# A cross-attention kernel whose engine calls are reissued in the order of a table, with 205 transfers on the other of two queues

## The chip, the cores and the metric

The kernel runs on one core of a Trainium2 chip. A core has a matrix engine (TensorE; PE in the profile, with PEld for its weight loads), a vector engine (VectorE, DVE), an activation engine (ScalarE, ACT), a general engine (GpSimd, POOL) and a synchronising engine (SyncE, SP) that here only issues transfers. Each takes its own instructions in order, and semaphores hold an instruction until what it needs is there. The metric is the device time of one execution in microseconds; smaller is better.

## The reference

A layer norm, a query projection, attention of 32 heads of width 32 over a context that serves as keys and as values, an output projection and a residual. Eight batches of 256 rows, model width 1024, all in float32:

```python
x = (hidden_states - mu) * jax.lax.rsqrt(var + LN_EPS) * ln_gamma + ln_beta
Q = _split_heads(x @ Wq.T)
scores = jnp.einsum('bhsd,bhtd->bhst', Q, K) * scale
scores = jnp.where(mask, scores, -jnp.inf)
probs = jax.nn.softmax(scores, axis=-1)
attn = jnp.einsum('bhst,bhtd->bhsd', probs, V)
out = attn @ Wout.T
return residual + out
```

## The kernel before

**Steps.** The loop (from L1204) has 64 steps `n`: eight batches by eight groups of four heads. Step `n` issues `scores(n + 1)` (L646), 8 matmuls of 32 rows of the array each, into the four tiles of the pool `ps_s`. `values` and `values_pair` (L823, L830) multiply the softmax of an earlier step with the values, 32 or 64 matmuls of 64 rows and 32 columns, into `ps_v`. Between them stand pieces of full-array work: query projections `pq` (`make_q` L504 with 256 columns; for batches 3 and up `query_product` L605, 16 matmuls of 128 columns for each of seven products, a Strassen-like scheme) and output projections `po` (`product_steps` L912, 512 columns). `pq` tiles live in `ps_q`, and `po` tiles mostly in `ps_o`; each of these pools has one buffer, so the next tile waits until ACT or DVE has copied the last one out. A table `PLAN` at the head of the file says at which step each load, sum and projection piece is issued.

**Softmax of a step** (`softmax_parts`, L670). For each head `j` and half `s` of the rows: DVE adds the mask and takes the minimum (L694), ACT takes the exponential and its sum (L698), DVE the reciprocal `rden` (L708). POOL multiplies (L714), or ACT for 52 of the 256 heads (L712). DVE transposes 32x32 blocks into `pT` (L720), ACT copies a part of them aside into `pc` (L726). Four transfers inside the chip then swap parts of `pT` (L800): two `pT<-pT`, and two `pT<-pc` that go back and wait for the first two. `values` reads the result.

**Head.** Thirty-two transposes of an identity (`busy`, L246) run while the first data arrive. The four quarters of `x` for batch 0 are the first loads on SP (`load_x`, L271), then `wq` block by block (`load_wq`, L333). DVE takes statistics of the quarters (L399), POOL raises to the power -1/2 (L407), DVE normalises (L425), PE transposes (L439), ACT and DVE copy (L448, L450), and `first_q` (L452, matmuls at L458) starts the projections.

**Tail.** After the loop the products of the last batch are added up (`end_steps`, matmuls at L997; `end_add`, L1003) and stored by `end_store` (L1353, issued at L1354), the last piece as 128 rows of 128 columns.

**Order and queues.** The whole body runs in a manual schedule (L241): every engine receives its instructions in the order in which Python makes the calls, and semaphores are derived from the same order. The identity and two small constants are written by POOL ahead of that line. `issue` (L254) puts a transfer on SP, or by `PLAN['qp']` on POOL at once or at the end of the step (L1337):

```python
        if mode == 0 or not in_loop:
            nc.sync.dma_start(to, of)
        elif mode == 1:
            nc.gpsimd.dma_start(to, of)
        else:
            at_end.append(partial(nc.gpsimd.dma_start, to, of))
```

Numbered in this order, the calls from L246 on are 6932: 3613 on PE, 1189 on DVE, 1016 on ACT, 636 on POOL (75 of them transfers) and 478 on SP (all transfers). On PE, a float32 matmul call becomes two weight loads and two matmuls.

Of the kernel before, what the change touches and what calls it, by code (L numbers as in the profile page):

```python
# [159 lines left out]
 'head': 1,  # L160
 'tail63': 1}

# [2 lines left out]

# [14 lines left out]
LN_EPS = 1e-5  # L180
MASKED = 3.0e38
NO_SCORE = 1.0e38


@with_exitstack
def xattn_kernel(
# [11 lines left out]
    nc = tc.nc  # L198
# [471 lines left out]
    def softmax_parts(n, copies=(), ahead=(), between=(), hooks={}, fill=()):  # L670
# [16 lines left out]
        def exps(j, part=range(NS)):  # L687
# [5 lines left out]
            for s in part:  # L693
                nc.vector.tensor_tensor_reduce(  # L694
                    out=e[:, s, :], in0=pss[j][:, s, :], in1=mbs[n // NQ], scale=1.0,
                    scalar=NO_SCORE, op0=ALU.add, op1=ALU.min, accum_out=mn[:, s : s + 1],
                )
# [312 lines left out]
    for n in range(N):  # L1010
        k = 0 if n == NQ + 1 else min(1, NQ * SPLIT - made)
# [14 lines left out]
    for b in range(1, B):  # L1026
        first = NQ * (b - 1) + 2
# [156 lines left out]
    for b in range(B - 1):  # L1184
        done, ends = 0, b == B - 2
# [19 lines left out]
    for n in range(N):  # L1205
        b, i = divmod(n - NQ, NQ)
# [194 lines left out]
    for cols in (first_cols, last_cols):  # L1401
# [2 lines left out]
        end_add(r01[:, cols], po)  # L1404
        end_store(0, 1, cols)


# [38 lines left out]
```

## Time and profile before

| | |
|---|---|
| median of 3 runs | 573.66 us (573.0 to 575.04) |
| span of the profiled execution | 572.0 us |
| instructions | 20001 |
| DMA engines | 116.93 MB, mean 204 GB/s |
| transfers issued by SP, packets' share of 16 engines | 55.2% |
| transfers issued by POOL, packets' share of 16 engines | 15.1% |

The span runs from the first to the last instruction of the profiled execution; no other time of that execution is given, and the lowest of the three runs lies 1.0 us above it. Rows of the profile read: line, engine, operation, what it writes `<-` what it reads, shapes and count, then busy time and mean duration in nanoseconds, then the idle time just ahead of these instructions with what ended most of it. A timeline row begins with its start and its length in us. A row of waits reads "who waited <- for whom: us in total, times, longest". A row of transfers ends with the size of one and the median time from issue to landing in us. "issue" is time in which an engine waited for nothing that the profile shows. Ends of matmuls are modelled; their starts are recorded.

### The profile page before, as it was taken

The page shows a single profiled execution, that of the slowest core. Times are in us where ns is not written, and L with a number is a line of the kernel's source. Part 1 is how long each engine was busy: PE and PEld are TensorE (multiplying, and loading weights), DVE is VectorE, ACT ScalarE, POOL GpSimd, SP SyncE. Part 2 cuts the span into 40 slices and gives each one's busy share as a digit, 9 for nine tenths or more (in the row PEclk, how much of TensorE's full clock was granted, in tenths as well). Part 3 has the DMA queues.
Part 4 walks back from the last instruction along what each step waited for, and adds up shares of the span by engine and source line. Part 5 has one row for each costly group of instructions (what it writes and reads, how often), then busy time and mean ns, then how long its engine had stood idle before and what let it go on. Part 6 is the DMA issues. An engine that isn't in the chain of part 4 may idle for free.

```text
span 572.0 us, 20001 instructions
## 1 busy us (share of the span) xinstructions
PE 562.9 (98%) x7162; PEld 394.6 (69%) x7162; DVE 466.2 (81%) x1701; ACT 450.5 (79%) x1527; POOL 399.1 (70%) x643
## 2 busy tenths in 40 slices
PE   8999999999999999999999999999999999999998
PEld 7788775767667677667675777667766777755454
DVE  5988899988878888988788987898877878688833
ACT  3699978888779877888768988789868888879920
POOL 1478978887678895787667774686955875267690
PEclk9999999999999999999999999999999999999999
DMA  8768778576777677877888677767866765547551
GB/s 298 278 174 252 203 206 230 133 205 189 203 235 203 205 207 220 257 210 205 214 249 234 206 201 221 229 200 209 233 189 193 226 182 175 145 136 228 153 167 74
DMA packets 45891, 116.93 MB, mean 204 GB/s; under 512 B 9136, under 2 KB 9904, under 8 KB 45792
## 3 DMA queue, kind: packets, MB, share of 16 engines
q1 hardware_dynamic: 38080, 90.14, 55.2%
q0 software_dynamic: 7424, 25.50, 15.1%
q8 instruction: 57, 0.93, 0.7%
q14 instruction: 42, 0.34, 0.2%
q10 hardware_dynamic: 288, 0.01, 0.0%
HBM read 64.23 MB, written 11.53 MB: 132 GB/s over the span
## 4 chain that ended last, share of the span: by engine, by line
PE 69%; DVE 9%; POOL 8%; ACT 6%; issue 4%; DMA 3%; SPq 0%; DVEq 0%; ACTq 0%; POOLq 0%
PE po_S L930 17%; PE pq_A L615 16%; PE sc L654 8%; PE pv L840 8%; PE po_A L930 8%; PE pq_S L615 6%; POOL e L714 5%; ACT e L698 3%; DVE e L694 3%; PE po_end L997 3%; DVE pT L720 3%; DMA pT<-pT 2%; ACT e L712 1%; PE pq L513 1%; DMA wq<-in_wq_dram 1%
## 5 line engine op out<-in xcount | busy, mean ns | idle before, releaser
L698 ACT ACTIVATE e<-e,mn 128x256 f32<-128x256 f32 x512 | 253.7, 502 | 32.8 <-DVE mn L694 30.2
L714 POOL TENSOR_SCALAR e<-e,rden 128x256 f32<-128x256 f32 x408 | 188.5, 476 | 125.0 <-DVE rden L708 116.8
L720 DVE STREAM_TRANSPOSE pT<-e 128x512 f32<-128x512 f32 x256 | 180.4, 707 | 54.6 <-POOL e L714 23.5
L694 DVE CUSTOM_DVE_ANT_0 e<-sc,mb 128x256 f32<-128x256 f32 x512 | 185.1, 415 | 13.0 <-PE sc L654 12.0
L726 ACT COPY pc<-pT 128x512 f32<-128x512 f32 x128 | 78.8, 617 | 43.7 <-DVE pT L720 28.5
L698 ACT ACTIVATION_READ_ACCUMULATOR e<-e,mn 128x1 f32 x512 | 98.9, 193 | 0.0
L513 PE MATMUL pq<-xnT,wq 128*128 128x256 f32 (+1 forms) x368 | 84.5, 383 | 0.0
L513 PEld LDWEIGHTS pq<-xnT,wq 128*128 128x128 f32 x368 | 68.6, 190 | 14.6 <-issue 3.4
L930 PE MATMUL po_S<-wo,at 128*128 128x512 f32 x152 | 73.5, 606 | 1.0 <-DVE r L972 0.7
L654 PE MATMUL sc<-k,qa 32*128 32x256 f32 x1024 | 73.8, 401 | 0.1
L654 PEld LDWEIGHTS sc<-k,qa 32*128 32x128 f32 x1024 | 45.9, 184 | 39.0 <-issue 17.8
L840 PE MATMUL pv<-pT,v_all 64*32 64x128 f32 x3584 | 61.0, 273 | 1.0 <-ACT e L712 0.6
L840 PEld LDWEIGHTS pv<-pT,v_all 64*32 64x32 f32 x3584 | 51.9, 105 | 12.8 <-issue 7.7
L930 PE MATMUL po_A<-wo,at 128*128 128x512 f32 x128 | 59.3, 604 | 0.1
L930 PE MATMUL po_S<-wo,s 128*128 128x512 f32 x104 | 49.9, 607 | 0.3 <-DVE rden L708 0.3
L708 DVE RECIPROCAL rden<-den 128x2 f32<-128x2 f32 x256 | 37.9, 148 | 13.1 <-ACT e L698 12.1
L712 ACT ACTIVATE e<-e,rden 128x256 f32<-128x256 f32 x104 | 46.8, 500 | 1.0 <-DVE rden L708 1.0
L615 PEld LDWEIGHTS pq_A<-xnT,wq 128*128 128x128 f32 x352 | 41.1, 192 | 5.6 <-issue 4.7
L930 PEld LDWEIGHTS po_S<-wo,at 128*128 128x128 f32 x152 | 26.0, 190 | 25.7 <-issue 23.9
L694 DVE DVE_READ_ACCUMULATOR2_ANT mn<- 128x1 f32 x512 | 42.3, 83 | 0.0
L615 PE MATMUL pq_A<-xnT,wq 128*128 128x128 f32 x352 | 41.2, 275 | 0.3 <-issue 0.3
L930 PEld LDWEIGHTS po_A<-wo,at 128*128 128x128 f32 x128 | 23.0, 189 | 26.5 <-issue 24.4
(116 smaller groups left out, 687.6 us busy)
## 6 DMA issues: line engine op xcount, KB each, us to landing
pT<-pT SPq DMA_DIRECT2D x128, 128.0 KB, 3.4
pT<-pc SPq DMA_DIRECT2D x128, 128.0 KB, 4.0
v_all<-in_kv_dram POOLq DMA_DIRECT2D x17, 512.0 KB, 4.8
k<-in_kv_dram SPq DMA_DIRECT2D x30, 256.0 KB, 4.2
r<-in_x_dram SPq DMA_DIRECT2D x26, 256.0 KB, 4.0
ring<-kept_T SPq DMA_DIRECT2D x11, 512.0 KB, 5.8
xnT<-xe SPq DMA_DIRECT2D x79, 64.0 KB, 3.9
out_dram<-r POOLq DMA_DIRECT2D x18, 256.0 KB, 3.7
```

What stands on the lines that cost most here:

```text
L513: nc.tensor.matmul(pqs[n], wq[:, o, c, :], xnTs[b](c), start=(c == 0), stop=(c == NC - 1),)
L615: nc.tensor.matmul(pqs[b][:, o, :], w[:, c], x_[:, c], start=begins and o + c == 0, stop=c == NK - 1, skip_group_check=True,)
L654: nc.tensor.matmul(scs[n][j][:, s, :], qa[r, n % NQ, ts(s, P)], ks[n - n % 2][r, n % 2, :], start=True, stop=True,)
L694: nc.vector.tensor_tensor_reduce(out=e[:, s, :], in0=pss[j][:, s, :], in1=mbs[n // NQ], scale=1.0, scalar=NO_SCORE, op0=ALU.add, op1=ALU.m ...
L698: nc.scalar.activation(e[:, s, :], e[:, s, :], AF.Exp, bias=mn[:, s : s + 1], scale=-1.0, accum_out=den[:, s : s + 1],)
L708: nc.vector.reciprocal(rden, dens[j])
L712: engine.activation(es[j][:, s, :], es[j][:, s, :], AF.Copy, scale=rden[:, s : s + 1])
L714: engine.tensor_scalar(es[j][:, s, :], es[j][:, s, :], rden[:, s : s + 1], 1.0, ALU.mult, ALU.mult,)
L720: nc.vector.transpose(pT[:, :, :, j, :, :].rearrange("p a i s k -> p (a i) s k"), es[j].rearrange("p s (b t) -> p b s t", t=K),)
L726: nc.scalar.copy(pc[:, :, ts(j, 2)], pT[:, 1, :, ts(j, 2)])
L840: nc.tensor.matmul(pvs[n][r][j * HD : (j + 1) * HD], vs[n - n % 2][ts(r, 2 * K), n % 2, i, ts(j, HD)], pT[ts(r, 2 * K), :, i, j, :, :], st ...
L930: nc.tensor.matmul(po, operand(b, name)[:, c], wo[:, which, c], start=begins and c == 0, stop=c == NK - 1, skip_group_check=not begins,)
```

## The change

Ahead of the kernel stand a table `ORDER`, a permutation of the numbers 0 to 6931 (runs written as `first-last`), and a dictionary `OTHER` of 205 call numbers with the engine that issues them instead. `Recorded` takes the place of `nc` right behind the manual schedule, keeps each call (engine, name, arguments) and issues none. After the last line of the body `issue` walks the table and makes the calls. The tiles are allocated in the same order as before, since Python runs the body as before. No call is added, left out or given other arguments.

By the table, against the old order of the same engine's calls, 1608 of 3613 calls on PE stand in another place, 950 of 1189 on DVE, 836 of 1016 on ACT, 443 on POOL and 260 on SP (of those that stay on their engine). A call on PE moves by at most 80 places.

Of the 205 transfers, 164 go from SP to POOL and 41 from POOL to SP:

| transfer | SP to POOL | POOL to SP |
|---|---|---|
| swaps `pT<-pT`, of 128 | 40 | 0 |
| swaps back `pT<-pc`, of 128 | 45 | 0 |
| blocks of x, `xnT<-xe` | 25 | 13 |
| keys `k`, values `v_all` and the last values in `wq` | 21 | 9 |
| residual rows `r` | 12 | 0 |
| `ring`, and `ring` kept in memory | 8 | 5 |
| weights `wq`, `wo` | 5 | 1 |
| rows `x`, mask | 3 | 2 |
| results `out` | 5 | 11 |

Among them are call 34, the first quarter of `x` for batch 0, and call 6931, the last store, both from SP to POOL.

```diff
+ORDER = """
+32-38 40 42 39 49 41 43-45 53-57 0-29 58-65 51 47 69-70 66-68 71-77 30-31 79-81 78 83-110 112 111 113 116-117
...
+6859 6904-6907 6898 6903 6913-6916 6806 6908-6911 6804 6917-6923 6902 6912 6924-6931
+"""
+OTHER = {
+    34: 'gpsimd', 46: 'gpsimd', 47: 'gpsimd', 48: 'gpsimd', 50: 'gpsimd', 51: 'gpsimd', 53: 'gpsimd',
...
+    6544: 'gpsimd', 6722: 'gpsimd', 6919: 'gpsimd', 6931: 'gpsimd',
+}
...
+class Recorder:
+    def __init__(self, engine, calls):
+        self.engine, self.calls = engine, calls
+
+    def __getattr__(self, name):
+        return lambda *a, **k: self.calls.append((self.engine, name, a, k))
+
+
+class Recorded:
+
+
+    def __init__(self, nc):
+        self.nc, self.calls = nc, []
+        for engine in ("tensor", "vector", "scalar", "gpsimd", "sync"):
+            setattr(self, engine, Recorder(engine, self.calls))
+
+    def __getattr__(self, name):
+        return getattr(self.nc, name)
+
+    def issue(self, order, other):
+
+        done = set()
+        for run in order.split():
+            first, *last = map(int, run.split("-"))
+            for i in range(first, (last[0] if last else first) + 1):
+                engine, name, a, k = self.calls[i]
+                getattr(getattr(self.nc, other.get(i, engine)), name)(*a, **k)
+                done.add(i)
+        assert len(done) == len(self.calls)
...
     ctx.enter_context(tc.manual_schedule())
+    nc = Recorded(nc)
...
+    nc.issue(ORDER, OTHER)
```

More of the change, by code (lines that the diff above doesn't have):

```diff
@@ new lines @@
+499 512 511 518 513-514 521 515 519 523-524 492 516-517 528 487 531-532 471-476 537-544 533 477-478 509 522
+591-592 525-527 529-530 536 535 593 598 390-391 485-486 488 490 545-576 534 577-579 581-582 580 583-588 597
+491 609 605-606 589-590 614 616 607-608 611 603-604 594 601-602 610 520 613 617 615 619-621 612 618 622 633
+596 595 600 599 637-680 717 624-626 623 627-631 697-698 632 689 685 687 696 699 686 690-693 688 709-710 704
+700 706 702 708 701 707 705 703 722 711-712 714 718-721 735-736 681-684 713 737 739 635 634 716 715 723 725
@@ new lines @@
+727 726 744-783 738 784 788-789 785-787 790-795 798 728 796 800 804 729 808-809 797 799 724 807 810 801 820
+817 811-813 815-816 845 839 842 695 848-850 945 732 802 949 636 694 740 818-819 741 829 822-823 814 825-826
+821 828 827 833 830-832 846-847 805 835 837 851-895 898-899 836 896-897 824 834 952-955 958 1034 909 838
+911-912 900-901 910 907 917-919 903 915-916 913-914 920-921 925 927-928 922-923 908 924 926 929-932 934-937
+956-957 959-966 1012 939 1016 1010 1039 1029 1217 841 803 904 1147 951 806 731 288 902 905 933 938 967-1009
@@ new lines @@
+5281 5330 5321-5322 5320 5318 5337-5339 5331 5336 5333 5332 5346 5342-5344 5355 5279 5334-5335 5340 5345
+5347-5348 5356-5432 5282 5141 5435 5454 5443-5444 5436-5438 5445 5447 5449-5451 5446 5452 5442 5453 5440 5448
+5456-5457 5441 5439 5341 5455 5459 5462 5472 5283 5484-5492 5434 5479 5460-5461 5483 5433 5458 5493-5509
+5511-5512 5463-5466 5468-5470 5482 5515-5516 5467 5471 5473-5474 5476 5286 5513-5514 5517 5519-5520 5518
+5526-5527 5523-5525 5530 5521-5522 5531 5528-5529 5535 5540 5534 5555-5556 5510 5546 5545 5547 5557 6455 5142
```

175 lines of the change are left out of this document (added).

## The prediction

> **What bounds the kernel now.** I read the cores' spans first, then busy times and the stretches of the span, then the matmul engine's waits, and only then the other engines and queues.
>
> ```profile
> core 0: 572.0 us, clock 1.000
> PE 562.9 (98%) x7162; PEld 394.6 (69%) x7162; DVE 466.2 (81%) x1701; ACT 450.5 (79%) x1527; POOL 399.1 (70%) x643
> ```
> ```profile
> 0.00:9.24 9.24, 6.66 (x40) 6.21 (x41) 4.49 (x10) 2.72 (x5) 1.47 (x9) 1.00 0.74 233
> 9.24:569.00 559.76, 556.00 (x7122) 388.36 (x7122) 461.39 (x1691) 447.75 (x1523) 397.67 (x635) 1.00 0.72 205
> 569.00:572.10 3.10, 0.19 (x2) 0.00 (x0) 0.29 (x1) 0.00 (x0) 0.00 (x0) 0.95 0.24 85
> ```
>
> The three stretches are the head (warm-up and first rows of x), the stream of matmuls, and the last store; the columns are length, busy PE, PEld, DVE, ACT, POOL, then clock, DMA share and GB/s. In the stream PE stands idle for 559.76 - 556.00 = 3.76 us, at full clock. The new table keeps every call, so it can take out idle time of PE, and move head and tail. It can't take out matmuls.
>
> ```profile
> 143.67 1.02 PE L930 MATMUL po_S<-wo,s 128*128 128x512 f32 x2
> 144.53 3.62 PE L513 MATMUL pq<-xnT,wq 128*128 128x256 f32 x16
> 148.81 1.13 PE L930 MATMUL po_S<-wo,at 128*128 128x512 f32 x2 [0.67 <-DVE r L972]
> ```
> ```profile
> 148.81 0.30 PEld L930 LDWEIGHTS po_S<-wo,at 128*128 128x128 f32 x2 [1.07 <-DVE r L972]
> PEld pq L513 <- issue: 3.4, 15, 0.3
> ```
>
> Here is one true stall (evacuation of `po_S` by DVE is late). PE shows 0.67 us. The weight loads, which otherwise pause 3.4 / 15 = 0.23 us in this group, pause 1.07, so the stall is about 0.84: the previous matmul's drawn end covers 0.17 of it. With the same cover of 0.17 on some 16 stalls in the stream, the 3.76 us become 3.76 + 16 x 0.17 = 6.5 us. Sixteen is a guess: the list of PE's waits names ten causes, two of them in the head. So the stall budget is 3.8 to 6.5 us; I take 6.5 as its whole size. The Trainium skill (Perfetto Trace Analysis, Tensor Engine Instruction) says that a matmul's end is estimated, not observed; the two rows at 148.81 agree. By drawn ends alone the budget would be 3.76 us.
>
> ```profile
> PE pq_A L615 <- issue: 1.3, 2, 1.0
> PE po_S L930 <- DVE r L972: 0.7, 1, 0.7
> PE pv L840 <- ACT e L712: 0.6, 1, 0.6
> ```
>
> Of it, 1.3 us (two pauses in `pq_A`) waits for nothing that the profile shows, and no order of ours addresses that. The addressable rest is at most 6.5 - 1.3 = 5.2 us, 0.9% of the span.
>
> **The change part by part.** I numbered the kernel's 6932 calls in the order it makes them, which is what the table's numbers mean, and counted. PE time between two calls is the sum, along an order, of each call's start-to-start time in the trace.
>
> *Order on PE.* 3613 calls, 1608 of them in another place. The 8 `scores` calls of a step and the 32 or 64 of `values` stay together; projection matmuls (`pq`, `po`) are cut into smaller pieces and spread. Stretches of small-tile work, each left and entered again, go from 69 to 71.
>
> ```profile
> 300.59 5.42 PE L930 MATMUL po_A<-wo,at 128*128 128x512 f32 x12
> 305.94 1.15 PE L654 MATMUL sc<-k,qa 32*128 32x256 f32 x16
> 307.02 1.98 PE L930 MATMUL po_A<-wo,at 128*128 128x512 f32 x4
> 308.84 3.40 PE L615 MATMUL pq_S<-sx,ring 128*128 128x128 f32 x29
> ```
>
> Each of these calls is two instructions. Six calls between two small-tile stretches take 305.94 - 300.59 = 5.35, two take 308.84 - 307.02 = 1.82 with one such border only. Four calls and a border are 3.53; at 0.86 a call (143.67 to 144.53 above) a border costs about 0.1, a stretch 0.2: two more cost 0.4 us. Cutting `pq` and `po` finer among each other costs nothing by these rows.
>
> What the cuts do is move waits. From the last `scores` matmul of a step to the first `values` matmul that needs its softmax, the PE time in between grows by over 0.5 us in 36 of 64 steps and shrinks by over 0.5 in 12 (at most 2.8). The one-buffer pool `ps_q` goes the other way: PE time between the last matmul into one tile and the first into the next was under 2 us once in 40, and is now in 11 (1.2 to 2.0). In that gap ACT must copy the tile out.
>
> ```profile
> L625 ACT ACTIVATE qa<-pq_S,qa 128x128 f32<-128x128 f32 x40 | 11.3, 366 | 0.4 <-PE pq_S L615 0.2
> L522 ACT ACTIVATE qa<-pq,qa 128x256 f32<-128x256 f32 x8 | 3.4, 462 | 0.0
> L698 ACT ACTIVATE e<-e,mn 128x256 f32<-128x256 f32 x512 | 253.7, 502 | 32.8 <-DVE mn L694 30.2
> ```
>
> A copy is 0.46 us, or 4 x 0.366 = 1.5 us for the four of a product, behind perhaps one exp of 0.5 us: it fits in 1.8 us where ACT comes to it at once, and is 0.2 us over where an exp and a product's four copies stand in line. Eleven such places cost 0 to 2.2 us; I take 1. Of the 5.2 us addressable I let the new distances remove 4.5, since they mostly lengthen. The stall term is -4.5 + 1 = -3.5 us; its ends are -5.2 (all addressable stalls gone) and +2.2 (none gone, all eleven late).
>
> *Order on DVE, ACT, POOL, SP.* 950, 836, 443 and 260 calls change place. Nothing is added; DVE at 81% and ACT at 79% hide behind PE as long as the distances above hold. I price it inside the stall term.
>
> *Transfers.* 164 go from SP to POOL, 41 back: 123 more on POOL, among them 85 of the 256 swaps of `pT` (L800).
>
> ```profile
> L261 POOL DMA_DIRECT2D v_all<-in_kv_dram x18 | 10.8, 600 | 0.0
> L1337 POOL DMA_DIRECT2D out_dram<-r x18 | 10.6, 586 | 0.3 <-issue 0.2
> L714 POOL TENSOR_SCALAR e<-e,rden 128x256 f32<-128x256 f32 x408 | 188.5, 476 | 125.0 <-DVE rden L708 116.8
> DVE pT L720 <- POOL e L714: 23.5, 67, 2.6
> ```
>
> 123 x 0.59 = 72.6 us more on POOL, 399.1 + 72.6 = 471.7 us (82%). It is hidden by POOL's 173 us of idle time, of which 116.8 wait for DVE's `rden`. If that cover is gone, the normalised `e` is late next, then DVE's transposes, the swaps and `values`.
>
> Two moved transfers have no cover. *Head:* the first quarter of x (call 34) goes from SP to POOL.
>
> ```profile
> 0.73 1.81 SPq L259 DMA_DIRECT2D x<-in_x_dram  x4
> 1.02 0.28 POOL masks.py:199 TENSOR_SCALAR_AFFINE_SELECT ring<-ring 128x128 f32<-128x128 f32 x1
> 3.58 1.47 DVE L399 BATCH_NORM_STATS2 st<-x 128x6 f32<-128x512 f32 x2 [3.58 <-DMA x<-in_x_dram]
> 9.24 0.57 PE L458 MATMUL pq<-xnT,wq 128*128 128x128 f32 x3 [1.04 <-DMA wq<-in_wq_dram]
> ```
> ```profile
> v_all<-in_kv_dram SPq DMA_DIRECT2D x7, 512.0 KB, 4.9
> v_all<-in_kv_dram POOLq DMA_DIRECT2D x17, 512.0 KB, 4.8
> r<-in_x_dram SPq DMA_DIRECT2D x26, 256.0 KB, 4.0
> r<-in_x_dram POOLq DMA_DIRECT2D x2, 256.0 KB, 6.5
> xnT<-xe SPq DMA_DIRECT2D x79, 64.0 KB, 3.9
> xnT<-xe POOLq DMA_DIRECT2D x17, 64.0 KB, 4.7
> out_dram<-x_again SPq DMA_DIRECT2D x1, 64.0 KB, 1.6
> ```
>
> DVE takes that quarter first in both orders. SP issued it at 0.73 and DVE began at 3.58. POOL is free at 1.30, 0.57 later, and from issue to landing a POOL transfer takes 0.8 us more (4.7 against 3.9), with ends -0.1 (4.8 against 4.9) and +2.5 (6.5 against 4.0). So DVE starts 1.4 us later (0.5 to 3.1). About 0.3 us of that is slack, because the first projection waited for `wq` too. After 9.24 PE has no idle time to absorb it: +1.1 us, ends +0.2 and +2.8. The Trainium skill (DMA: Bandwidth & Descriptors, Specifications) gives about 1 us to the first byte on GpSimd's path and 0.6 on SP's; the pair 4.7 and 3.9 agrees in sign. By an estimate from that page the head would cost 0.57 + 0.4 - 0.3 = 0.7 us. *Tail:* the last store (call 6931, 64 KB, 1.6 us on SP) is issued by POOL: by the same pairs +0.8 us, ends -0.1 and +2.5.
>
> *Sum* against the profiled execution: 572.0 - 3.5 (stalls) + 0.4 (stretches) + 1.1 (head) + 0.8 (tail) = 570.8 us. The median of the runs shown, 573.66, lies 1.7 above that span, so I forecast 570.8 + 1.7 = **572.5 us**. This case, stalls mostly gone and about half of that given back at both ends, spans 571.0 to 574.5.
>
> **The rivals.** *The table pays in full:* the 5.2 us go, head and tail hide (by the `v_all` pair, POOL is no slower). For it: 36 longer distances. Against: POOL is free 0.57 us late whatever the queue does. 573.66 - 5.2 + 0.4 = 568.9.
>
> *Stalls move, none goes:* each wait removed comes back in `ps_q`, stall term 0. For it: 11 gaps under 2 us with ACT 79% busy; against: ACT is reordered too. 573.66 + 2.3 = 576.0.
>
> *POOL becomes the bound (the slower side).* Place: a `pT` swap on POOL that stands ahead of `e` and waits.
>
> ```profile
> SPq L800 <- DMA pT<-pT: 103.8, 66, 5.3
> SPq L800 <- ACT pc L726: 55.5, 22, 4.2
> SPq L800 <- ACT e L698: 50.2, 25, 8.5
> SPq L800 <- ACT at L853: 34.6, 10, 7.4
> ```
>
> SP waits 244.1 us over 256 swaps, 0.95 each. If POOL waits as long for its 85, that is 81 us: 471.7 + 81 = 552.5. Head and tail, where POOL has nothing to do, are 10.9 us (9.24 - 1.47 and 3.10). It decides once POOL's remaining waits for `rden`, 116.8 us now, stay above 572.0 - 552.5 - 10.9 = 8.6 us. If a sixth stays (19.5), the span is 552.5 + 10.9 + 19.5 = 582.9, with the 1.7 around it 584.6. For it: behind 17 of the 45 returning swaps on POOL the table puts under 3 us of POOL work between the two swaps of a step, less than a landing. Against: 28 have more, and the longer PE distances allow it.
>
> *The order does not arrive:* if the instruction order of the program were remade behind the table, 573.7. Against: the kernel builds in a manual schedule, and today's trace follows its calls one by one.
>
> **How the numbers follow.** Forecast 0.38, full gain 0.17, stalls move 0.22, POOL bound 0.20, no effect 0.03. A measurement of this kernel tells about 0.3% (1.7 us) from no change: faster is below 571.9, slower above 575.4. Faster: 0.17 of the full gain and 0.17 of the forecast's lower part; same: 0.20 of the forecast, 0.03 of moved stalls, 0.03 of no effect; slower: 0.01, 0.19 and 0.20. So 0.34, 0.26, 0.40. The range 568.3 to 582.0 leaves out the upper part of the POOL case and the least of the full gain, under 0.2 together.
>
> **What would show it.** Stall term: PE idle in the long stretch near 1.5 to 2.5 us instead of 3.76, with `ps_q` copies named where it remains. Head: DVE's first statistics near 5.0 instead of 3.58, the first projection near 10.3 instead of 9.24. Tail: last matmul to end of span about 0.8 us longer. POOL busy near 472 us, PE still at full clock. I am wrong if PE idles more than 6 us in the stream, if waits for POOL's `e` grow well over 23.5 us on DVE, or if the first statistics start as early as now.

## The result, and the profile after

The changed kernel takes 592.38 us (median of 4 runs, 590.88 to 594.14), the kernel before 573.33 in the runs beside it: a ratio of 1.0318, with a 95% interval of 1.0273 to 1.0364. It is slower by about 19 us. Here and below, medians and ratios leave out executions that took over 1.5% more than the fastest of the same kernel: one of start_back (594.02 us) and one each of queues_only and both_back (about 1988 us, over twice the others, which nothing here explains). The profiled execution spans 591.2 us where the one of before spans 572.0.

First the spans and the busy time of the engines, from the view of cores and the page:

```profile
core 0: 591.2 us, clock 0.994
PE 573.6 (97%) x7162; PEld 401.6 (68%) x7162; DVE 460.1 (78%) x1701; ACT 452.5 (77%) x1527; POOL 464.8 (79%) x766
```

POOL has its 123 transfers more (x766 for x643) and 65.7 us more work. No engine but PE is near the span. Now the same three stretches as before the change, cut at the first projection and behind the last addition (columns: length, busy PE, PEld, DVE, ACT, POOL, clock, DMA share, GB/s):

```profile
0.00:11.55 11.55, 7.61 (x40) 7.13 (x40) 3.87 (x9) 1.79 (x3) 2.71 (x10) 1.00 0.76 268
11.55:588.00 576.45, 566.00 (x7122) 394.47 (x7122) 456.24 (x1693) 450.66 (x1525) 461.57 (x755) 0.99 0.69 197
588.00:591.30 3.30, 0.00 (x0) 0.00 (x0) 0.00 (x0) 0.00 (x0) 0.54 (x1) 1.00 0.21 76
```

The head is 11.55 - 9.24 = 2.3 us longer, the stream 576.45 - 559.76 = 16.7. In the stream PE is idle for 576.45 - 566.00 = 10.45 us (3.76 before), and "busy" for 10 us more on the same 7122 matmuls. A part of that is matmuls at half clock, in two windows of 3.4 us that the kernel before doesn't have:

```profile
96.97:100.38 3.41, 3.41 (x64) 2.27 (x65) 2.18 (x12) 2.46 (x8) 1.95 (x4) 0.51 0.56 129
455.40:458.80 3.40, 3.40 (x9) 1.24 (x5) 2.03 (x7) 3.17 (x13) 2.50 (x6) 0.50 0.64 212
```

They account for up to half of their 6.8 us, 3.4. The rest is drawn ends that cover stalls. So I also measured stalls by starts: for each run of like matmuls, the time from its start to the next run's start, less what undisturbed runs of that kind take in the trace of before (0.858 us a `po` call, 0.432 and 0.223 a `pq` call of 256 and 128 columns, 1.08 the scores of a step, 1.09 the values of one). Behind the first 16 us these excesses sum to 6.6 us before and 21.6 after: 15.0 us of new stalls, half clock included, in some two dozen places.

The waits that the prediction named, and the ones that grew most (engine and line, what it waited for, us in total, times, longest):

```profile
POOL e L410 <- DVE rden L410: 50.1, 61, 6.9
DVE rden L410 <- ACT e L410: 47.6, 78, 2.2
DVE pT L410 <- POOL e L410: 31.8, 54, 2.4
POOL pT L410 <- DMA pT<-pT: 15.5, 8, 5.7
```
```profile
DVE rden L708 <- ACT e L698: 12.1, 21, 1.0
```

The last row is of before. All calls now have one line, L410, because the helper issues them. DVE waits four times as long for ACT's exponentials, and POOL, which waited 116.8 us for `rden`, now waits 50.1 for it and is held by swaps instead.

How a stall comes about is best seen at two places. The first, from the timelines of SP and of PE:

```profile
85.23 0.58 SPq L410 DMA_DIRECT2D wo<-in_woT_dram  x1
85.91 0.58 SPq L410 DMA_DIRECT2D pT<-pT  x1
89.96 0.51 SPq L410 DMA_DIRECT2D pT<-pc  x1
90.56 0.53 SPq L410 DMA_DIRECT2D v_all<-in_kv_dram  x1
91.19 0.38 SPq L410 DMA_DIRECT2D k<-in_kv_dram  x1
91.62 0.51 SPq L410 DMA_DIRECT2D xnT<-xe  x1
92.23 0.55 SPq L410 DMA_DIRECT2D pT<-pc  x1
```
```profile
94.59 0.40 PE L410 MATMUL pv<-pT,v_all 64*32 64x128 f32 x2
96.91 1.94 PE L410 MATMUL pv<-pT,v_all 64*32 64x128 f32 x62 [1.92 <-DMA pT<-pc]
```

The last returning swap of step 7 is issued at 92.23, behind transfers of `v_all`, `k` and `xnT`, and lands at 96.8. The values of step 7 start at 94.59, break off, and lose 2.2 us. The half-clock window begins at 96.97. The second place shows a flipped transfer holding POOL:

```profile
134.48 0.56 POOL L410 DMA_DIRECT2D x<-in_x_dram  x1
138.17 0.54 POOL L410 DMA_DIRECT2D k<-in_kv_dram  x1 [3.13 <-PE sc L410]
138.74 1.84 POOL L410 TENSOR_SCALAR e<-e,rden 128x256 f32<-128x256 f32 x4
```
```profile
139.71 0.71 DVE L410 STREAM_TRANSPOSE pT<-e 128x512 f32<-128x512 f32 x1 [3.02 <-DMA pT<-pT]
```
```profile
141.45 0.91 ACT L410 ACTIVATE e<-e,rden 128x256 f32<-128x256 f32 x2 [2.65 <-DVE rden L410]
142.76 0.46 ACT L410 ACTIVATE qa<-pq,qa 128x256 f32<-128x256 f32 x1
```
```profile
139.51 1.88 PE L410 MATMUL po_S<-wo,at 128*128 128x512 f32 x4
143.27 3.72 PE L410 MATMUL pq<-xnT,wq 128*128 128x256 f32 x16 [1.88 <-ACT qa L410]
```

The load of `k` (call 1419, on SP before) waits on POOL for the scores that still read the buffer. Behind it stand the products `e` of step 14; then DVE idles 3.0 us (the profile names a swap that landed at the same time), ACT 2.7, and the copy that frees the bank of `ps_q` starts at 142.76, 3 us behind the matmuls that filled it. PE stands in front of `pq_20`.

Last, where the slack went. For each of the 64 steps I took from the traces the times along the way from the last scores matmul to the first values matmul. Medians in us:

| | before | after | order_timed | pe_new | heads_back |
|---|---|---|---|---|---|
| last scores to end of last `pT` transpose | 8.7 | 11.9 | 11.9 | 10.6 | 11.6 |
| to end of last copy `pc` | 0.7 | 1.5 | 1.4 | 0.7 | 1.4 |
| to issue of last swap `pT<-pT` | 0.6 | 1.5 | 1.2 | 0.6 | 1.4 |
| to its landing | 2.9 | 3.3 | 3.3 | 2.9 | 3.0 |
| to issue of last swap `pT<-pc` | 0.4 | 1.4 | 1.1 | 0.4 | 1.9 |
| to its landing | 3.4 | 3.6 | 3.2 | 2.8 | 3.0 |
| left until the first values matmul | 10.6 | 3.6 | 4.6 | 10.8 | 3.8 |
| scores to values in all | 26.4 | 29.7 | 30.0 | 30.4 | 29.5 |
| steps with under 1 us left | 1 | 11 | 8 | 0 | 9 |

The other columns belong to experiments below. The distance from scores to values did grow, by 3.3 us, but every link of the way in between grew too, and 7 of the 10.6 us of slack are gone. That this is what costs the 19 us is not shown by the table: pe_new keeps its slack and loses about as much.

### The profile page after: what moved, and what is told of

Same layout as the page of the kernel before. It is cut to its first block, busy times and chain, and to the rows that moved or that the text cites. A ratio compares the mean times of both kernels' runs of the same rounds, so it can differ in the third digit from the quotient of the medians.

```text
span 591.2 us, 20072 instructions
## 1 busy us (share of the span) xinstructions
PE 573.6 (97%) x7162; PEld 401.6 (68%) x7162; DVE 460.1 (78%) x1701; ACT 452.5 (77%) x1527; POOL 464.8 (79%) x766
## 4 chain that ended last, share of the span: by engine, by line
PE 45%; POOL 13%; DMA 12%; DVE 11%; ACT 9%; issue 8%; SPq 2%; POOLq 0%; DVEq 0%; ACTq 0%
PE pq L410 7%; PE po_A L410 7%; PE po_S L410 7%; ACT e L410 6%; POOL e L410 6%; PE pv L410 6%; PE sc L410 6%; PE pq_A L410 5%; DMA pT<-pc 4%; DMA pT<-pT 4%; DVE pT L410 4%; DVE e L410 3%; PE pq_S L410 3%; PE po_end L410 2%; SPq L410 2%
## 5 line engine op out<-in xcount | busy, mean ns | idle before, releaser
L410 ACT ACTIVATE e<-e,mn 128x256 f32<-128x256 f32 x512 | 255.6, 501 | 32.8 <-DVE mn L410 26.1
L410 POOL TENSOR_SCALAR e<-e,rden 128x256 f32<-128x256 f32 x408 | 190.5, 478 | 53.4 <-DVE rden L410 50.1
L410 DVE STREAM_TRANSPOSE pT<-e 128x512 f32<-128x512 f32 x256 | 176.9, 702 | 45.1 <-POOL e L410 31.8
L410 DVE CUSTOM_DVE_ANT_0 e<-sc,mb 128x256 f32<-128x256 f32 x512 | 190.9, 410 | 6.9 <-PE sc L410 4.7
L410 ACT COPY pc<-pT 128x512 f32<-128x512 f32 x128 | 77.7, 612 | 35.0 <-DVE pT L410 20.4
L410 ACT ACTIVATION_READ_ACCUMULATOR e<-e,mn 128x1 f32 x512 | 97.0, 189 | 0.0
L410 PE MATMUL pq<-xnT,wq 128*128 128x256 f32 (+3 forms) x400 | 91.9, 377 | 2.3 <-ACT qa L410 1.9
L410 PEld LDWEIGHTS pq<-xnT,wq 128*128 128x128 f32 x400 | 71.7, 190 | 21.8 <-issue 8.4
L410 PE MATMUL sc<-k,qa 32*128 32x256 f32 x1024 | 78.7, 402 | 1.6 <-DVE mn L410 0.6
L410 DVE RECIPROCAL rden<-den 128x2 f32<-128x2 f32 x256 | 38.0, 153 | 49.0 <-ACT e L410 47.6
L410 PE MATMUL po_S<-wo,at 128*128 128x512 f32 x152 | 72.2, 600 | 0.0
L410 PEld LDWEIGHTS sc<-k,qa 32*128 32x128 f32 x1024 | 48.7, 184 | 28.8 <-issue 10.6
L410 PE MATMUL pv<-pT,v_all 64*32 64x128 f32 x3584 | 62.4, 275 | 4.4 <-DMA pT<-pc 3.5
L410 PEld LDWEIGHTS pv<-pT,v_all 64*32 64x32 f32 x3584 | 52.3, 106 | 17.1 <-issue 7.3
L410 PE MATMUL po_A<-wo,at 128*128 128x512 f32 x128 | 62.7, 624 | 1.0 <-DVE qa L410 0.9
L410 ACT ACTIVATE e<-e,rden 128x256 f32<-128x256 f32 x104 | 48.5, 500 | 14.4 <-DVE rden L410 14.4
L410 PE MATMUL po_S<-wo,s 128*128 128x512 f32 x104 | 49.9, 601 | 0.0
L410 PEld LDWEIGHTS pq_A<-xnT,wq 128*128 128x128 f32 x352 | 42.3, 192 | 10.1 <-issue 8.1
L410 PE MATMUL pq_A<-xnT,wq 128*128 128x128 f32 x352 | 43.8, 277 | 0.2 <-ACT qa L410 0.2
L410 DVE DVE_READ_ACCUMULATOR2_ANT mn<- 128x1 f32 x512 | 42.5, 83 | 0.0
L410 PEld LDWEIGHTS po_A<-wo,at 128*128 128x128 f32 x128 | 23.5, 197 | 27.5 <-issue 25.4
L410 PEld LDWEIGHTS po_S<-wo,at 128*128 128x128 f32 x152 | 26.5, 190 | 23.0 <-issue 22.0
```

What stands on the lines that cost most here:

```text
L410: getattr(getattr(self.nc, other.get(i, engine)), name)(*a, **k)
```

## The experiments

Each ratio is against runs of the kernel before on the same chip. Every kernel keeps all 6932 calls. `ORDER` is the table of the change and `OTHER` its dictionary of engines.

**The parts by call number: recorded, order_only, queues_only.**

The first edit makes queues_only, the second order_only, and both together recorded, which issues every call where the kernel before does.

```diff
 ORDER = """
-32-38 40 42 39 49 41 43-45 53-57 0-29 58-65 51 47 69-70 66-68 71-77 30-31 79-81 78 83-110 112 111 113 116-117
...
+0-6931
 """
```
```diff
 OTHER = {
-    34: 'gpsimd', 46: 'gpsimd', 47: 'gpsimd', 48: 'gpsimd', 50: 'gpsimd', 51: 'gpsimd', 53: 'gpsimd',
...
-    6544: 'gpsimd', 6722: 'gpsimd', 6919: 'gpsimd', 6931: 'gpsimd',
 }
```

> The recorder alone: the table is 0 to 6931 in order and no transfer changes its queue. Both theories: the same time as the kernel before, 573 +- 1.5 us, span 572, since neither the order nor a queue changes. If it is over 576, something in recording itself (tiles allocated ahead of all calls) costs time, and both theories have to share less than 19 us.

Measured: 574.25 us, ratio 0.9999 (0.9974 to 1.0023). Recording the calls and issuing them later costs nothing that these runs can show.

> The new order, with all 205 transfers on their old queues. Theory 'queues' (transfers on POOL land later and hold POOL up while they wait for earlier swaps; the order itself is good): 569 to 576 us, PE idle in the stream 2 to 5 us. Theory 'order' (the new order leaves too little PE time for what must happen in between, above all for copies out of the one-buffer tiles): 584 to 590 us, the long PE waits for ACT and DVE (1.9 us for qa and the like) still there, and only the 2.8 us of the head and the 0.9 us of the tail gone.

Measured: 660.02 us, ratio 1.148 (1.140 to 1.156).

> The old order, with the 205 transfers on their new queues. Theory 'queues': 585 to 592 us, nearly all of the loss, with PE waits for pT<-pc and with POOL waits for pT<-pT of the kind of the 15.5 us seen in the changed kernel. Theory 'order': 576 to 579 us, head (+2.8 us) and tail (+0.9 us) and little else. Over 592 would say that the two parts help each other: POOL's swaps stand right behind each other in the old order, and the new order had made room for them.

Measured: 755.99 us, ratio 1.314 (1.306 to 1.322). Either half alone is far worse than both together, so neither theory holds as put. A part of both losses is clock: it was 0.953 over the 655.4 us of order_only's profile and 0.920 over the 750.2 of this one, so up to 31 and 60 us of them are lost clock. From the waits of queues_only:

```profile
DVE pT L251 <- POOL e L251: 135.1, 130, 9.0
POOL pT L251 <- DMA pT<-pT: 66.2, 27, 6.9
```

In the old order the two swaps of a step follow each other, so on POOL the second holds everything behind it until the first has landed. That is the mechanism of my slower rival, and here it is on view; in the changed kernel the wait for the landing is 15.5 us. But these two kernels were not fair: a call number says nothing of where in the other queue a flipped transfer belongs. The next pair mends that.

**The head and the tail on the old queue: ends_back.**

```diff
 OTHER = {
-    34: 'gpsimd', 46: 'gpsimd', 47: 'gpsimd', 48: 'gpsimd', 50: 'gpsimd', 51: 'gpsimd', 53: 'gpsimd',
+    46: 'gpsimd', 47: 'gpsimd', 48: 'gpsimd', 50: 'gpsimd', 51: 'gpsimd', 53: 'gpsimd', 219: 'gpsimd',
...
-    6544: 'gpsimd', 6722: 'gpsimd', 6919: 'gpsimd', 6931: 'gpsimd',
+    6544: 'gpsimd', 6722: 'gpsimd', 6919: 'gpsimd',
 }
```

> The changed kernel, with two transfers put back on SP: the first quarter of x (call 34) and the last store (call 6931). Both theories: DVE's first statistics at 3.6 us again instead of 6.8, the last store 0.9 us shorter, so 3.7 us less than the changed kernel, 588.7 us (587.5 to 590). If the head gains under 1 us, other transfers at the head (wo, wq, v_all on POOL beside it) hold the first projection.

Measured: 592.52 us, ratio 1.0317 (1.0269 to 1.0366); no gain, where 588.7 us was expected. Its timeline of the head:

```profile
1.33 0.89 POOL L410 DMA_DIRECT2D wo<-in_woT_dram  x1 [0.37 <-issue]
3.38 0.69 DVE L410 BATCH_NORM_STATS2 st<-x 128x6 f32<-128x512 f32 x1 [3.38 <-DMA x<-in_x_dram]
11.23 2.02 PE L410 MATMUL pq<-xnT,wq 128*128 128x128 f32 x13 [2.19 <-DMA wq<-in_wq_dram]
```

The statistics start as early as before the change, but the first projection only at 11.23: it now waits 2.19 us for the first block of `wq`, which SP issued at 2.57, as early as before the change (2.58). The new order sends `wo` ahead of it, at 1.33 (16.82 before), so I read this as `wq` sharing the DMA engines with a load that nobody waits for yet; that was not tried by itself.

**Order and queues at their proper places: order_timed, queues_timed.** The engines' orders as in order_only and queues_only, but a transfer that changes queue stands there by the time at which the trace of its own order issued it. SyncE's calls around the load of `k` for step 16 (1419), from order_only to order_timed, and GpSimd's, from queues_only to queues_timed:

```diff
-1421 1835 1355 1561 1419 1553 1626
+1561 1354 1418 1558 1419 1417 1553
```
```diff
-1394-1395 1402-1403 1419 1430 1432-1433 1533-1534
+1403 1430 1432-1433 1419 1533-1534 1540-1541
```

> The new order on all five engines with none of the 205 transfers flipped, but unlike order_only each transfer stands in its old queue (SyncE's or GpSimd's) at the place that the trace of the changed kernel gives it by the time at which it was issued there; the order within every engine's other work is the new one. 270 of SyncE's 478 calls stand at another place than in order_only, by up to 9. 'Queues' theory (the loss comes from transfers that GpSimd issues late and is held by): 570 to 577 us, with PE idle back at 9 to 11 us. 'Order' theory (the new order of the engines leaves too little between scores and values, wherever the transfers are issued): 585 to 596 us, with the median time left between the landing of a step's last swap and its first values product near the changed kernel's 3.6 us and not the old kernel's 10.6. 'Misfit' (SyncE is too full for these transfers in this order, whatever place they get): above 600, as in order_only (660), with SyncE's waits for pT<-pT above 150 us.

Measured: 589.21 us, ratio 1.0265 (1.0217 to 1.0313), inside the 'order' theory's range, with the slack that it named (4.6 us in the table).

> The old order on every engine with the 205 transfers flipped, but each flipped transfer stands in its new queue at the place that the trace of the kernel before gives it by time; 479 of GpSimd's 759 calls stand elsewhere than in queues_only, by up to 12. 'Queues' theory: 580 to 600 us, with GpSimd's waits for transfers 20 us or more. 'Order' theory: 572 to 580 us. 'Misfit' (two swaps of one step that wait for each other's landing hold GpSimd in the old order, wherever they stand): above 640 us (queues_only: 757), with DVE's waits for GpSimd's e above 60 us (135 there).

Measured: 612.34 us, ratio 1.0643 (1.0593 to 1.0693), above 'queues' and below 'misfit', so none of the three. Some 70 of the 86 us of order_only were my placing. The new order without any flipped transfer already loses most of what the change loses; the 205 flips add about 3 us to it (589.21 to 592.38), which the overlapping intervals don't tell from nothing, though in the old order they cost 39. In the changed kernel POOL stands 46 us in front of flipped transfers, by the gaps ahead of them in its timeline (34 of over 0.05 us; queues_timed also 46, queues_only 191).

**TensorE alone: pe_new.**

TensorE's calls stand in the new order, all others in the old, with no flips. TensorE's calls around the scores of step 31 (3317 to 3324), from the kernel before to pe_new:

```diff
-3243-3264 3313-3314 3317-3340
+3232-3255 3317-3324 3313 3256-3264 3314 3325 3327-3328 3326 3329
```

> TensorE alone in the new order; VectorE, ScalarE, GpSimd and SyncE in the old one, and none of the 205 transfers flipped. In the changed kernel the median from a step's last scores product to the end of its last pT transpose was 11.9 us (8.7 before), and the way from there to the landing of the last swap 11.9 us in place of about 8. 'Chain' theory (it is the feeding engines' new order and queues that lengthen this way and eat the slack; TensorE's order alone gives the steps 2 us more): 569 to 576 us, the way to the pT transposes back at 8 to 9.5 us. 'TensorE order' theory (its sequence itself asks for tiles too early, as in the eleven gaps below 2 us of the ps_q bank): 584 to 594 us, with waits for qa copies above 5 us. 'Misfit' (orders of engines that were not made for each other wait for each other in turn): above 600 us.

Measured: 591.37 us, ratio 1.0297 (1.0262 to 1.0332). In the table above its steps keep their slack (10.8 us) and still it is 17.7 us slower, at other places:

```profile
PE sc L393 <- DVE qa L393: 2.7, 2, 2.2
PE po_S L393 <- DVE r L393: 1.8, 1, 1.8
```

The last of these stalls can be followed back, in the timelines of ACT, DVE and PE:

```profile
149.06 0.77 ACT L393 COPY at<-pv 128x128 f32<-128x128 f32 x4 [2.25 <-PE pv L393]
150.84 0.17 DVE L393 RECIPROCAL rden<-den 128x2 f32<-128x2 f32 x1 [2.75 <-ACT e L393]
151.75 0.65 DVE L393 TENSOR_TENSOR r<-po_S,r 128x512 f32<-128x512 f32 x1
152.46 1.12 PE L393 MATMUL po_S<-wo,at 128*128 128x512 f32 x2 [1.79 <-DVE r L393]
```

ACT stands in front of copies of `pv`, which TensorE computes from 146.86 to 148.9, while the exponentials behind these copies are ready (DVE took their minima from 146.2 on). DVE then waits for an exponential, behind that stands the addition that empties `po_S`, and PE waits for it. So here an engine in its old order waits for a result of TensorE, and in the end TensorE waits for that engine. In total ACT waits twice as long for `pv` as in the kernel before (first row pe_new, second before):

```profile
ACT at L393 <- PE pv L393: 23.5, 9, 9.2
ACT at L853 <- PE pv L840: 11.2, 9, 6.0
```

The 'chain' theory falls as a theory of the whole loss. The time is in the range of 'TensorE order', but its sign didn't quite come: PE idles 4.5 us for `qa` in all, of ACT or DVE, not over 5, and only 1.2 of it in front of `pq`, where the short gaps are. How much of the 17.7 us comes about as in this chain is not shown.

**The start alone, and mends of the stream: head_new, pool_mend, pe_mend, all_mend.**

The table of head_new ends in the old order behind call 218, and its dictionary behind 53:

```diff
 ORDER = """
...
+211-212 82 52 219-6931
 """
 OTHER = {
     34: 'gpsimd', 46: 'gpsimd', 47: 'gpsimd', 48: 'gpsimd', 50: 'gpsimd', 51: 'gpsimd', 53: 'gpsimd',
...
-    6544: 'gpsimd', 6722: 'gpsimd', 6919: 'gpsimd', 6931: 'gpsimd',
 }
```

One of the 31 moves of pool_mend on GpSimd, around 1419:

```diff
-1561 1634 1419 1534 1533 1540-1541 1565 1553
+1634 1534 1533 1540-1541 1419 1565 1553
```

One of the five of pe_mend on TensorE (the values of step 7, 1068 to 1099, go behind three calls of `po`), and four of its 75 copies on ScalarE (5439 to 5442, ahead of exponentials):

```diff
-1060-1101 1104 1102-1103
+1060-1067 1100-1101 1104 1068-1099 1102-1103
```
```diff
-5348 5444 5436 5438 5450 5446 5452 5442 5453 5440 5448 5457 5441 5439
+5348 5442 5440-5441 5439 5444 5436 5438 5450 5446
```

> The kernel before with only its first 219 calls (to the first step's softmax) in the new order, and of the 205 flipped transfers only the seven among them: 34 (first quarter of x), 46, 50, 51 (wq), 47 (k), 48 (v_all) and 53 (wo), on GpSimd. In the changed kernel the first projection started at 11.55 us instead of 9.24 and the warm-up 1.1 later. 'The head's delay stays' : 575.5 to 577.5 us, 2 to 3.5 above the kernel before. 'The head's delay is taken up by the stream behind it' (putting 34 back alone took 2.9 us from one profiled span and nothing from the median): 573 to 574.7 us.

Measured: 578.8 us, ratio 1.0096 (1.0076 to 1.0116): 5.5 us, above both cases, and so closer to 'the head's delay stays'. Of it, PE's trace shows 3.2 us at the first projection and about 1.7 in a half-clock window that begins there (the window's row, then PE's timeline):

```profile
12.00:15.40 3.40, 3.40 (x17) 3.14 (x16) 2.59 (x8) 1.88 (x5) 2.69 (x5) 0.50 1.03 414
```
```profile
12.48 3.43 PE L221 MATMUL pq<-xnT,wq 128*128 128x128 f32 x16
```

> The changed kernel with 31 calls of GpSimd moved ahead, in its own order alone, into times at which GpSimd stood waiting in front of a transfer and they were ready (97 of its 759 calls stand elsewhere). In the changed kernel's trace GpSimd stood 46 us in front of flipped transfers (34 times over 0.05 us); so at 135.0 us, 3.1 us in front of the load k_16 (call 1419), with the products of step 14 ready behind it: VectorE then idled 3.0 us, ScalarE 2.7, the copy of pq_19 came late and TensorE stood 2.05 us in front of pq_20. 'Held GpSimd' theory: the stall at pq_20 goes and so does part of the rest, 584 to 589 us. 'Tight order' theory (holds only decide where the lack of slack shows): 590 to 594.

Measured: 590.99 us, ratio 1.0304 (1.0276 to 1.0331). The stall at `pq_20` is gone: `pq` follows `po_S` at once.

```profile
137.17 0.59 POOL L464 DMA_DIRECT2D k<-in_kv_dram  x1 [0.45 <-PE sc L464]
```
```profile
138.51 1.88 PE L464 MATMUL po_S<-wo,at 128*128 128x512 f32 x4
140.23 3.62 PE L464 MATMUL pq<-xnT,wq 128*128 128x256 f32 x16
```

So the chain from the held load to PE was read rightly; but the kernel's time stays inside the changed kernel's interval, as the 'tight order' theory had it.

> The changed kernel with five units of TensorE's order (values of steps 7, 20 and 52, scores of steps 31 and 51) moved 0.9 to 2.6 us later, behind work that stood ready, and 75 copies of PSUM results on ScalarE and VectorE moved ahead into times at which those engines waited. Queues unchanged. The stalls at the five units came to 3.1, 0.95, 1.1, 2.1 and 1.2 us, with 1.3 and 0.8 more in two stretches of half clock behind them. 'A few tight places' theory: most of that goes, 581 to 586 us. 'No slack anywhere' theory: stalls come up at other places, 589 to 594.

Measured: 590.38 us, ratio 1.0324 (1.0281 to 1.0368). The values of step 7 no longer break off (first two rows), but a block of scores now does, at 143.45, 2.6 us from its start to its second part:

```profile
95.59 2.84 PE L460 MATMUL po_A<-wo,at 128*128 128x512 f32 x6
98.36 1.16 PE L460 MATMUL pv<-pT,v_all 64*32 64x128 f32 x64
...
143.45 0.70 PE L460 MATMUL sc<-k,qa 32*128 32x256 f32 x4
146.04 1.81 PE L460 MATMUL sc<-k,qa 32*128 32x256 f32 x12 [1.88 <-DVE mn L460]
```

> Both edits of pool_mend and pe_mend in one kernel. 'A few tight places': 577 to 583 us, about the sum of the two gains. 'No slack anywhere': 588 to 594.

Measured: 592.09 us, ratio 1.0309 (1.0276 to 1.0343). 'A few tight places' falls, since all three kernels stay at the changed kernel's time. In pe_mend one stall went and another came, as above.

**The heads inside a step, and the start put back: heads_back, heads_new, start_back, both_back.**

The first edit is of heads_back: the minima and reciprocals of step 9 on VectorE (heads 0, 1, 0, 3, r0, 1, 2, 3, r1, 2, r2, r3 before it, 0, 0, 1, 1, r0, 2, 2, 3, r1, 3, r2, r3 with it). The second is of start_back, whose table begins with the calls 0 to 218, each engine's in the old order. heads_new mixes the heads in the old order in the same way; both_back has both edits.

```diff
-1012 1016 1010 1029 1024 1018 1022 1027 1031 1020 1036 1042
+1010 1012 1016 1018 1024 1020 1022 1027 1031 1029 1036 1042
```
```diff
 OTHER = {
-    34: 'gpsimd', 46: 'gpsimd', 47: 'gpsimd', 48: 'gpsimd', 50: 'gpsimd', 51: 'gpsimd', 53: 'gpsimd',
```

> The changed kernel with the order of the four heads inside each step put back, on VectorE, ScalarE and GpSimd: every kind of call (minimum, exponential, reciprocal, product with it, transpose, copy) keeps the places that the new order gives it among the other calls, and those places are filled head by head as in the old order (448, 416 and 184 calls move). The old order takes both halves of head 0, then of head 1, and so on; the new one mixes them (in step 9 VectorE takes the minima of heads 0, 1, 0, 3, then 1, 2, 3, 2), so that no head is complete early. 'Mixed heads' theory: this is why the way from a step's last scores to its last pT transpose took 11.9 us in place of 8.7 (medians) and VectorE waited 47.6 us for ScalarE's e in front of rden (12.1 before): 580 to 586 us, with the way at 9 to 10.5 us and that wait below 25. 'TensorE order' theory (what TensorE asks for and when decides, and the heads inside a step do not): 588 to 594, with the way above 11.

Measured: 591.66 us, ratio 1.0281 (1.0238 to 1.0323). DVE's wait for ACT in front of `rden` fell from 47.6 to 30.7 us, the way to the last transpose only from 11.9 to 11.6:

```profile
DVE rden L463 <- ACT e L463: 30.7, 57, 1.8
```

> The kernel before with the new order's mixing of the heads inside a step, in the 50 of 64 steps where it fits between the other calls' old places (781 calls of VectorE, ScalarE and GpSimd move); all else old. 'Mixed heads' theory: 578 to 584 us, the way from scores to the last transpose above 10.5 us. 'TensorE order' theory: 573 to 576, since the old order leaves 10.6 us (median) between the last swap's landing and the values products to take it up.

Measured: 612.67 us, ratio 1.0652 (1.061 to 1.0693): far above both cases, so it tells nothing for the 'mixed heads' theory, which heads_back has refuted as the main cause. Changing the order inside an engine at places made for another order cost 38 us here.

> The changed kernel with its first 219 calls in the old order and on the old queues, and all the rest in the new order with its 198 other flipped transfers. head_new, which is the opposite, cost 5.5 us. If the start and the stream add: 586 to 588.5 us. If the stream's lack of slack takes up what the start gives (as with call 34 alone): 590 to 594.

Measured: 584.8 us, ratio 1.0173 (1.0110 to 1.0236), an interval clear of the changed kernel's (1.0273 to 1.0364). It rests on three runs that spread from 582.07 to 588.65. By these the start and the stream add: the start is worth about 8 us here, 5.5 by head_new, which has the tighter interval.

> start_back with the heads inside each step put back too. 'Mixed heads' theory and start adding: 575 to 581 us. 'TensorE order' theory with the start adding: 586 to 589; with nothing adding: 590 to 594.

Measured: 590.45 us, ratio 1.0203 (1.0117 to 1.0289), three runs from 583.36 to 591.21. None is in the 575 to 581 of 'mixed heads'; the interval is too wide to say more.

**TensorE's order in parts: spacing_back, scores_back, spacing_new_feeders.**

Each block of scores (and, but for scores_back, of values) stands behind as much projection work as in the old order. Around step 31, from pe_new to spacing_back and scores_back, and alike from the changed kernel to spacing_new_feeders:

```diff
-3317-3324 3313 3256-3264 3314 3325 3327-3328 3326 3329
+3313 3256-3264 3314 3317-3325 3327-3328 3326 3329-3340
```

> pe_new with TensorE's scores and values put back to where the old order has them, measured by the projection work issued ahead of them; only the order of the projections among themselves is new (464 of TensorE's 3613 calls stand elsewhere than in the old order, 1436 elsewhere than in pe_new). All else old, as in pe_new. 'Placement' theory (TensorE's loss comes from where the scores and values stand among the projections): 573 to 577 us. 'Projections' theory (it comes from the order of the projections, with the ps_q bank's short gaps): 585 to 592, as pe_new.

Measured: 584.78 us, ratio 1.0201 (1.0156 to 1.0246): just under the 'projections' range. 464 of 3613 calls out of their old place, projections alone, are enough for 10.8 us, with slack near that of before (9.4 us, one step under 1).

> pe_new with the scores alone put back in that way; values and projections stay in the new order. By TensorE's time the new order's steps 30 to 59 start their scores 4.7 to 13.2 us apart (standard deviation 2.05), the old order's 6.6 to 10.9 (1.14); VectorE has about 7.2 us of work for a step (460 us for 64). 'Uneven scores' theory (scores that follow closely wait for VectorE to free the banks): 574 to 580 us. 'Values' theory (it is the values that ask too early): 586 to 592.

Measured: 606.96 us, ratio 1.0561 (1.0524 to 1.0599), far above both cases. That speaks for neither: like heads_new, the kernel mixes places of one order with places of another.

> The changed kernel, with its feeders and queues as they are, but TensorE's scores and values put back as in spacing_back. 'Placement' theory, if the feeders' new order can serve the old places: 576 to 584 us. If orders made for each other must stay together ('misfit'): 600 us or more. If neither placement nor fit matters: 590 to 594.

Measured: 629.21 us, ratio 1.0966 (1.0926 to 1.1006): in the 'misfit' range. The old places of scores and values lose 37 us more than the new ones when the feeders follow the new order.

No kernel of the study beats the one before.

## Why the prediction was wrong, step by step

The forecast was 572.5 us and a small gain from fewer stalls of TensorE; the measured kernel takes 592.38, with more stalls.

- *What bounds the kernel.* Right: PE, with 3.8 to 6.5 us of stalls. By starts the whole was 6.6.
- *Stretches, +0.4.* Too small to be seen beside the rest.
- *Tail, +0.8 (-0.1 to +2.5).* Right. From the end of DVE's last addition to the end of the span it is 3.5 us, 2.5 before (first row after, second before):

```profile
587.44 0.29 DVE L410 TENSOR_TENSOR x_again<-po_end,x_again 128x128 f32<-128x128 f32 x1 [0.33 <-PE po_end L410]
```
```profile
569.23 0.29 DVE L1003 TENSOR_TENSOR x_again<-po_end,x_again 128x128 f32<-128x128 f32 x1 [0.34 <-PE po_end L997]
```

- *Head, +1.1 (+0.2 to +2.8).* The place was right, the middle too small: 2.3 us at the first projection in the changed kernel, still inside the range, but 5.5 for the whole start by head_new. The step that was mis-sized is "POOL is free at 1.30 ... DVE starts 1.4 us later": DVE started 3.2 us later.

```profile
1.30 0.70 POOL L410 DMA_DIRECT2D x<-in_x_dram  x1 [0.35 <-issue]
2.12 0.31 POOL masks.py:199 TENSOR_SCALAR_AFFINE_SELECT ring<-ring 128x128 f32<-128x128 f32 x1
2.36 0.77 POOL L410 DMA_DIRECT2D wo<-in_woT_dram  x1
6.78 1.29 DVE L410 BATCH_NORM_STATS2 st<-x 128x6 f32<-128x512 f32 x2 [6.78 <-DMA x<-in_x_dram]
```

  The quarter of x landed 6.78 - 1.30 = 5.5 us behind its issue, against 3.58 - 0.73 = 2.85 on SP. I had priced it as 0.8 more; that is 2.6 more, just past my upper end of 2.5. The transfer also went ahead of the operation that makes the identity, so the warm-up began 1.1 us later. And I costed call 34 alone and not `wo`, which the new order moves ahead of the first `wq`; in ends_back, with call 34 back on SP, the projection still starts only at 11.23, behind `wq`.
- *Stall term, -3.5 (-5.2 to +2.2).* This is the step that decided, and it had the wrong sign: +15.0 us of stalls by starts. It failed at "I let the new distances remove 4.5, since they mostly lengthen". They did lengthen: scores to values by 3.3 us in the median. But a distance is slack only less the way that has to fit in it, and that way rests on the sentence "Nothing is added; ... I price it inside the stall term", for the 950, 836, 443 and 260 moved calls of DVE, ACT, POOL and SP. By the medians of the table its links sum to 16.7 us before and 23.2 after: 3.2 more to the transposes, 0.8 to the end of the copies, 0.9 and 1.0 in the queues ahead of the two swaps. Nothing in the text priced that. The sum also left out what pe_new shows, where the slack stays and the stalls come all the same: an engine that TensorE feeds waits for TensorE, and TensorE then waits for it. So the step is refuted by the stalls, and the loss of slack is one way to them and not shown to be the main one. The term's upper end didn't allow it either: it counted eleven `ps_q` gaps as the only new stalls. One of them is the stall at `pq_20`; it came not because the gap is short in itself, but because ACT was held from POOL.
- *POOL becomes the bound, 584.6.* POOL's work was predicted (471.7, measured 464.8), and its waits were put at 81 us for the swaps alone and are 46 in front of all flipped transfers. But POOL still waits 50.1 us for `rden`, and most of the loss is there without any flipped transfer (order_timed, 1.0265). The 584.6 was the nearest number to the result, on a mechanism that pays at most some 3 of the 19 us: luck, as far as it came near. Of the other rivals, 'stalls move' had it right that the stalls don't go, but not that new ones come on top.
- *Signs named.* PE idle in the stream "over 6 us" and waits for POOL's `e` above 23.5 (31.8) both came, as signs that I'm wrong; the clock fell as well, which I had not expected.

What the runs show of the 19 us: about 5.5 are the start (head_new), 1 the tail, at most some 3 the flips, and the stream's other 10 or so are there when TensorE follows the new order, with the old feeders (pe_new, 17.7 us) or with the new (order_timed, 15.5 with the start). Whether it is the same loss in both is not shown, since the places differ. What stays open is which property of the new order costs these. Slack between swap and values went, yet pe_new has it and is no faster; mixed heads and the largest stalls were each tried and are not the main cause, and for uneven scores no kernel here decides. Of pe_new's 17.7 us, 10.8 are there with the order of the projections alone (spacing_back). The kernels that put an order of TensorE beside feeders of another, or mixed heads at old places (spacing_back, pe_new, scores_back, heads_new, spacing_new_feeders), run 11 to 55 us above the kernel before, so such parts can't be priced one by one; I take the old orders to be fitted to each other, as the chain at 152.46 in pe_new suggests, which is a reading and not shown for the whole.

## What to carry to other kernels

A reordering is priced along the whole chain that must fit into a distance, and on every engine and queue of it: a longer distance between producer and consumer on the bound engine says nothing until the links in between are added up. In these runs the orders of in-order engines belonged together: test a part of such a table by swapping stretches of the program (here its first 219 calls), since swapping one engine's order, or moving transfers without placing them by time, may measure the misfit instead. At the head, look at every load that is moved ahead of the first one that the bound engine waits for, and not only at the load that changes queue.

## What the hardware showed that I had not expected

- Stalls of about 2 us on PE were followed by a window of 3.41 us at half clock in some cases and not in others: in the changed kernel 1.92 us of idle time at 95.0 were and 1.88 at 141.4 were not; in pe_new 2.37 and 2.11 were (windows at 447.18 and 563.23) and 2.23 was not. What decides it is not shown. Each window is worth up to 1.7 us. Several kernels of the study had one at the end of a late head. The profile of the kernel before, which never idles so long in the stream, has none there, but seven of its 47 executions beside the experiments show a granted clock of 0.996 or 0.997, about what one such window makes, and took 575.82 to 578.22 us, where the rest took 572.05 to 576.28. So the clock is a part of why executions of one kernel differ (pe_mend: 588.24 us at 0.999, 595.4 at 0.991); the loss itself is not the clock, since pe_mend's execution at 588.24 has no window in the stream.
- The same 256 KB took 5.5 us to land from POOL's queue and 2.85 from SP's, at the head where both queues were filling. Over the whole changed kernel POOL's medians were longer by 0.9 to 1.0 us for `v_all` of 512 KB, `k` and `xnT`, by 0.2 to 0.5 for the swaps and `r`, and shorter by 0.7 for the results `out`. The 0.8 of the prediction was fair for these, and the first quarter of x was not one of them.
- The same 205 flips cost 182, 39 or at most some 3 us, by the order that they stand in and their places in it.
